# Sigmoid attention in bursts of seven energy tiles, with the values eight tiles behind

## The chip, the cores and the metric

The kernel runs on one core of a Trainium2 chip. The metric is device time in microseconds from the first to the last instruction of the program; lower is better. A core has a matrix engine (TensorE, "PE" in the profile, its weight loads "PEld"), a vector engine (VectorE, "DVE"), an engine for activation functions (ScalarE, "ACT"), a general one (GpSimd, "POOL"), and a sequencer that issues transfers ("SP"). Matmuls write to PSUM, which has eight banks of 512 float32 per partition; everything else lives in SBUF, with 128 partitions.

## The reference

The input x has 4 images of 64 channels and 96 x 96 positions (9216). Two layers follow one another, each added to its own input; `_gn` normalizes groups of two channels.

```python
q = einsum('bchw,oc->bohw', x, wq) + bq      # 8 channels
k = einsum('bchw,oc->bohw', x, wk) + bk      # 8 channels
v = einsum('bchw,oc->bohw', x, wv) + bv      # 64 channels
energy = einsum('bcn,bcm->bnm', Q, K)        # 9216 x 9216 per image
att = sigmoid(energy)
out = einsum('bcm,bnm->bcn', V, att) + x
scale = sigmoid(mlp(mean(out)) + mlp(max(out)))
layer0 = out * scale
...
x = x + layer0(_gn(x))
x = x + layer1(_gn(x))
```

Layer 1 takes a two-dimensional Fourier transform of the normalized x, multiplies the 32 x 16 lowest frequencies by a complex 64 x 64 matrix each (the spectral weights), and transforms back.

## The kernel before

The four images are two pairs p; the 64 channels of a pair's two images fill 128 partitions. The attention of a pair is cut into 18 blocks of 512 queries (NBLK), so there are 36 blocks in all. The keys are cut into 72 chunks of 128 (NCH). One **tile** is the energies of one chunk of one image against the block's 512 queries: a matmul (L424) with 32 contracted rows and 128 columns of weights that fills one PSUM bank. Queries and keys are held in four groups of 32 rows, and successive tiles take successive groups (`r = 32 * (t % 4)`). A block has 144 tiles. A sigmoid on ScalarE (L428) turns energies in PSUM into attention in SBUF (`at`). Then each **pair** of tiles (one chunk, both images) is multiplied by the values `vT` (L435): two matmuls of 64 columns each, which fill the two halves of the output `acc`, one bank, over all 72 chunks. Values and attention are full float32, which the profile shows as two matmul records, two passes, per matmul; the energies are float32r, one record.

The work is cut into **bursts** of six tiles (BURST), 24 a block, 864 in all. Six PSUM banks hold the energies, as two tensors `eb[0]`, `eb[1]` of three banks (PART); one sigmoid works on each. The loop over bursts t does: energies of burst t+1 and their two sigmoids, the side work listed in `mid[t]`, the three value pairs of burst t, the next block's queries in the fourth burst from a block's end, and the side work in `end[t]`; after a block's last burst, two vector instructions add `acc` to x and take a maximum (L578, L580). The remaining two PSUM banks form the pool `ps_a`: one holds `acc`, the other is used by side work, through `bank_a`.

Side work is all that isn't attention. In block 0 it makes keys and values of pair 0 a chunk of 512 at a time; in blocks 1 to 13 it takes statistics of pair 1 and normalizes it; in block 17 it makes pair 1's keys and values. From block 18 on, layer 1 of pair 0 runs as side work (class `Hidden`): `result` (combine with the gate, L158), `transposes` (L262), `along_w` (L272), `stats_steps`, `along_h` (L299), `mix` (L199), `back_h` (L318) and `back_w` (L339). Each is put at a fixed burst by `place(offset, every, steps)`. For `mix`, the weights of four of the 32 frequency rows are loaded into four buffers (`l1.weights`, L310) every ten bursts from burst 100 of pair 1 on; `mix(q, 0)` follows six bursts later and `mix(q, 1)` three after that. Each `mix(q, 1)` also stores its result (L215). After the attention, layer 1 of pair 1 runs as a tail, with nothing beside it.

The order in which instructions stand on each engine's queue follows the program's order, save where the framework that places them takes one that it reckons to be ready ahead of one that isn't. `later` keeps a step behind a marked vector instruction on its engine. Semaphores are put in by the framework from what each instruction reads and writes.

Of the kernel before, what the change touches and what calls it, by code (L numbers as in the profile page):

```python
# [33 lines left out]
F32 = mybir.dt.float32  # L34
F32R = mybir.dt.float32r
AF = mybir.ActivationFunctionType
ALU = mybir.AluOpType
AX = mybir.AxisListType
PSUM = bass.MemoryType.PSUM

P = 128
B, C, H, W = 4, 64, 96, 96
N = H * W
NPAIR = B // 2
# [3 lines left out]
KH = 32  # L48
NB = 512
NBLK = N // NB  # L50
NCH = N // P
BURST = 6
PART = 3
BURSTS = 2 * NCH // BURST
SIDE = 4
U = KH * KW * 4
UPAD = 4 * SIDE
STRIP = 8 * W
SQ = 32
NSQ = H // SQ  # L60
NSTRIP = N // STRIP
# [16 lines left out]
def tile_kernel(ctx: ExitStack, tc: tile.TileContext, x, cst, late, spec, out):  # L78
    nc = tc.nc
# [10 lines left out]
    xs = []  # L90
    for p in range(NPAIR):
        xt = xpool.tile([P, N], F32, tag=f"x{p}", name=f"x{p}")
        for s in range(9):
            cols = bass.ts(s, N // 9)
# [137 lines left out]
    class Hidden(Layer1):  # L232
# [25 lines left out]
        def transposes(self, r):  # L258

            pt = self.bank(f"pt_{self.p}_{r}")  # L260
            for i in range(4):
                nc.tensor.transpose(pt[:W, bass.ts(i, P)], xs[self.p][:, bass.ts(4 * r + i, W)],  # L262
                                    ident)
            self.xts[r] = self.work.tile([W, NB], F32, tag="xT", bufs=5, name=f"xT_{self.p}_{r}")
            self.move(self.xts[r], pt[:W, :])

        def along_w(self, m):
# [78 lines left out]
    with tc.tile_pool(name="work", bufs=1) as work, \  # L346
            tc.tile_pool(name="kv", bufs=1) as kvp, \
            tc.tile_pool(name="q", bufs=2) as qp, \
            tc.tile_pool(name="att", bufs=2) as attp, \
            tc.tile_pool(name="ps_s", bufs=1, space=PSUM) as ps_s, \  # L350
            tc.tile_pool(name="ps_a", bufs=2, space=PSUM) as ps_a:

        eb = [ps_s.tile([P, PART, NB], F32, tag=f"e{i}", name=f"e{i}") for i in range(2)]

        kT = kvp.tile([P, NCH // 2, P], F32R, tag="kT", name="kT")

        def bank_a(name):
            return ps_a.tile([P, NB], F32, tag="a", name=name)

        def halves(src, bias, name):  # L360

# [7 lines left out]
        mark = [None]  # L369
# [6 lines left out]
        def later(step):  # L376
            with tc.issue_after(mark[0].ins):
                step()
# [12 lines left out]
        def values_of(p, s):  # L391
            pp = bank_a(f"pv_{p}_{s}")
            for i in range(4):
                nc.tensor.matmul(pp[:, bass.ts(i, P)], xs[p][:, bass.ts(4 * s + i, P)],  # L394
                                 named("wv"), start=True, stop=True)
            nc.vector.tensor_tensor(  # L396
                vT[:, 4 * s:4 * s + 4, :], pp.rearrange("p (i m) -> p i m", m=P),
                named("bv").unsqueeze(1).to_broadcast([P, 4, P]), ALU.add)
# [16 lines left out]
                    nc.vector.tensor_copy(q[to:to + 32, cols], q[of:of + 32, cols])  # L415
            return q

        def energies(p, n, g, q):


            for i in range(BURST):
                t = BURST * g + i
                r = 32 * (t % 4)
                nc.tensor.matmul(eb[i // PART][:, i % PART, :], kT[r:r + 32, t // 4, :],  # L424
                                 q[r:r + 32, :], start=True, stop=True)
            at = attp.tile([P, BURST, NB], F32, tag="att", name=f"at_{p}_{n}_{g}")
            for h in range(BURST // PART):
                nc.scalar.activation(at[:, bass.ts(h, PART), :], eb[h], AF.Sigmoid)  # L428
            return at

        def attend(acc, g, at):
            for i in range(BURST):
                j, b = (BURST * g + i) // 2, i % 2
                half = slice(b * C, (b + 1) * C)
                nc.tensor.matmul(acc[half, :], vT[:, j, half], at[:, i, :],  # L435
                                 start=(j == 0), stop=(j == NCH - 1))

        def stats_of(p):

# [43 lines left out]
        q = queries(0, 0)  # L483
# [2 lines left out]
        keys(0, 1)  # L486
        values_of(0, 1)

        T = NPAIR * NBLK * BURSTS
        mid = [[] for _ in range(T)]  # L490
        end = [[] for _ in range(T)]
        for s in range(2, NBLK):
            end[s - 2] += [lambda s=s: keys(0, s)]
            mid[s - 1] += [lambda s=s: values_of(0, s)]
            if s + 1 < NBLK:
                end[s - 2] += [lambda s=s: later(norm0[s + 1])]
        each, norm1, mv1 = stats_of(1)
        for i, step in enumerate(each + norm1):
            end[(2 + i // 3) * BURSTS + 2] += [lambda step=step: later(step)]
        last = (NBLK - 1) * BURSTS  # L500
        for s in range(NBLK):
            t = last + -(-(4 * s + 1) // 3)
            end[t] += [lambda s=s: keys(1, s)]
            mid[t + 1] += [lambda s=s: values_of(1, s)]

        first = NBLK * BURSTS

        def place(offset, every, steps):
            for i, step in enumerate(steps):
                end[first + offset + every * i] += [lambda step=step: later(step)]  # L510

        gate, steps, _ = after(0)
        place(2, 2, steps)
        l1 = Hidden(0, gate, bank_a, lambda dst, src: nc.vector.tensor_copy(dst, src), work)  # L514
        x1d = dram.tile([P, N], F32, tag="x1", name="x1d")
        place(9, 3, [lambda s=s: (l1.result(s), nc.sync.dma_start(
            x1d[:, bass.ts(s, STRIP)], xs[0][:, bass.ts(s, STRIP)])) for s in range(NSTRIP)])
        place(13, 2, [lambda r=r: l1.transposes(r) for r in range(H // 4)])
        place(22, 8, [lambda m=m: l1.along_w(m) for m in range(H // 16)])
        place(64, 2, l1.stats_steps())  # L520

        def workspace():
            ws = xpool.tile([P, N], F32, tag="x0", name="ws")
            l1.ut = ws[:, :U + UPAD]
            at = 2080
            l1.wts = [ws[:, at + 1024 * i:at + 1024 * (i + 1)] for i in range(4)] * (KH // 4)
            l1.vms = [ws[:, at + 4096:at + 5120]] * (KH // 4)
            l1.z = ws[:, at:at + 3072].rearrange("q (h m) -> q h m", m=P)

        place(76, 1, [workspace])  # L530
        place(80, 4, [lambda i=i: l1.along_h(i) for i in range(4)])
        place(98, 1, [l1.constant_mode])
        place(100, 10, [lambda q=q: l1.weights(range(4 * q, 4 * q + 4)) for q in range(KH // 4)])
        for half in range(2):
            place(106 + 3 * half, 10, [lambda q=q, half=half: l1.mix(q, half)
                                       for q in range(KH // 4)])
        place(200, 3, [lambda i=i: l1.back_h(i // 4, i // 2 % 2, i % 2) for i in range(8)])
        place(244, 3, [lambda i=i: l1.back_w(i, x1d) for i in range(H // 4)])


        early = []
# [4 lines left out]
            for i, w in enumerate(early):  # L546
                nc.gpsimd.dma_start(w, spec[NSLOT + i])

        place(340, 1, [fetch])
        again = vT.rearrange("p j m -> p (j m)")  # L550
        for s in range(NSTRIP):
            end[T - BURSTS + 2 * s + 1] += [lambda s=s: nc.sync.dma_start(
                again[:, bass.ts(s, STRIP)], xf[bass.ts(1, P), bass.ts(s, STRIP)])]

        at = energies(0, 0, 0, q)
        qn = None
        for t in range(T):
            p, n, g = t // (NBLK * BURSTS), t // BURSTS % NBLK, t % BURSTS
            nxt = None
            if t + 1 < T:  # L560
                p1, n1, g1 = (t + 1) // (NBLK * BURSTS), (t + 1) // BURSTS % NBLK, (t + 1) % BURSTS
                if g1 == 0:
                    q = qn
                nxt = energies(p1, n1, g1, q)
            for step in mid[t]:
                step()
            if g == 0:
                acc = bank_a(f"acc_{p}_{n}")
            attend(acc, g, at)
            at = nxt  # L570
            if g == BURSTS - 4 and t + 4 < T:
                m = t // BURSTS + 1
                qn = queries(m // NBLK, m % NBLK)
            for step in end[t]:
                step()
            if g == BURSTS - 1:
                blk = xs[p][:, bass.ts(n, NB)]
                nc.vector.scalar_tensor_tensor(blk, acc, 1.0, blk, ALU.mult, ALU.add,  # L578
                                               accum_out=sums[p][:, n:n + 1])
                mark[0] = nc.vector.tensor_reduce(maxs[p][:, n:n + 1], blk, AX.X, ALU.max)  # L580
        gate, steps, f = after(1)
        for step in steps:
            step()
# [2 lines left out]
    with tc.tile_pool(name="tail", bufs=1, reuse_waits="tile") as tail, \  # L586
# [49 lines left out]
        for s in range(NSTRIP):  # L636
# [9 lines left out]
                pa = pa_bank.tile([P, 2 * NB], F32, tag="a", name=f"pa_{n}", bufs=2)  # L646
            v = xt.rearrange("q (h n c) -> q n h c", n=NSQ, c=SQ)
            for k in range(NSQ):
                last = nc.tensor.matmul(pa[:, bass.ts(i, STRIP // NSQ)], fw[:, bass.ts(k, P)], v[:, k],  # L649
                                 start=(k == 0), stop=(k == NSQ - 1))  # L650
            if i < NSTRIP // NSQ - 1:
                continue

# [73 lines left out]
        z = tail.tile([P, P, SQ], F32, tag="z", name="z_1")  # L727
        for i in range(4):
            for b in range(2):
                nc.vector.transpose(z[:H, b * C + i * NO:b * C + (i + 1) * NO, :], pz[b][i][:H, :].rearrange(  # L730
                    "q (k o) -> q o k", o=NO))
        banks.close()
        py_bank = psum("ps_y", 2)
        occupy(2, last, py_bank)
# [100 lines left out]
```

## Time and profile before

| what | value |
| --- | --- |
| time, median of 3 runs | 3196.64 us (3194.6 to 3197.18) |
| span of the profiled execution | 3196.5 us |
| mean granted TensorE clock | 0.995 |
| first energy matmul | 29.9 us after the start |
| last value matmul ends | 3106.0 us |
| ScalarE, of which idle before sigmoids | 2432.9 us busy, 682.8 us idle |
| VectorE busy | 396.4 us |

A line of the profile's groups reads: line of the kernel, engine, operation, tiles written and read, shapes, count, then busy time in us and the mean length of one in ns, then idle time of the engine before it and what ended it. A matmul's length is from its start to a modelled end, and matmuls overlap, so two of them take less than the sum. A line of the timeline reads: start in us, length in us of the merged instructions, then as above. Windows give, for each stretch, the busy time of each engine with the instruction count, the granted clock, the share of the transfer engines and GB/s.

### The profile page before, as it was taken

The page shows a single profiled execution, that of the slowest core. Times are in us where ns is not written, and L with a number is a line of the kernel's source. Part 1 is how long each engine was busy: PE and PEld are TensorE (multiplying, and loading weights), DVE is VectorE, ACT ScalarE, POOL GpSimd, SP SyncE. Part 2 cuts the span into 40 slices and gives each one's busy share as a digit, 9 for nine tenths or more (in the row PEclk, how much of TensorE's full clock was granted, in tenths as well). Part 3 has the DMA queues.
Part 4 walks back from the last instruction along what each step waited for, and adds up shares of the span by engine and source line. Part 5 has one row for each costly group of instructions (what it writes and reads, how often), then busy time and mean ns, then how long its engine had stood idle before and what let it go on. Part 6 is the DMA issues. An engine that isn't in the chain of part 4 may idle for free.

```text
span 3196.5 us, 39125 instructions
## 1 busy us (share of the span) xinstructions
PE 3153.5 (99%) x17490; PEld 1070.9 (34%) x17490; DVE 396.4 (12%) x838; ACT 2432.9 (76%) x1765; POOL 24.5 (1%) x49
## 2 busy tenths in 40 slices
PE   6999999999999999999999999999999999999998
PEld 3333333333333333334333333333333333333336
DVE  4200000000000000002331100000000111000015
ACT  3688888888888888886677777777777777888871
POOL 0000000000000000000000000000000000000001
PEclk9999999999999999999999999999999999999998
DMA  3000000000000000000120100121020102100026
GB/s 139 1 1 1 1 1 1 1 1 1 1 1 1 1 1 1 1 1 1 37 92 17 40 1 30 63 89 37 13 28 10 40 30 70 66 1 1 6 62 221
DMA packets 39145, 88.63 MB, mean 28 GB/s; under 512 B 10336, under 2 KB 17248, under 8 KB 38880
## 3 DMA queue, kind: packets, MB, share of 16 engines
q1 hardware_dynamic: 31856, 61.88, 6.4%
q0 software_dynamic: 5344, 19.27, 1.7%
q10 hardware_dynamic: 1776, 4.97, 0.4%
q8 instruction: 137, 2.24, 0.3%
q14 instruction: 32, 0.26, 0.0%
HBM read 62.77 MB, written 23.33 MB: 27 GB/s over the span
## 4 chain that ended last, share of the span: by engine, by line
PE 98%; DVE 1%; DMA 1%; issue 0%; ACT 0%; POOL 0%; SPq 0%; ACTq 0%
PE acc L435 74%; PE e L424 18%; PE pv L394 1%; PE pv L199 1%; PE py L339 1%; PE pq L405 1%; PE pk L385 1%; DMA x<-in_x_dram 0%; PE py L742 0%; PE pt L262 0%; DVE x L158 0%; DVE xt L641 0%; PE pz L318 0%; PE pu L299 0%; PE pa L272 0%
## 5 line engine op out<-in xcount | busy, mean ns | idle before, releaser
L428 ACT ACTIVATE at<-e 128x1536 f32<-128x1536 f32 x1728 | 2412.6, 1448 | 682.8 <-PE e L424 682.7
L435 PE MATMUL acc<-at,vT 128*64 128x512 f32 x10368 | 2418.1, 601 | 0.0
L435 PEld LDWEIGHTS acc<-at,vT 128*64 128x64 f32 x10368 | 667.8, 136 | 1294.7 <-issue 1279.3
L424 PE MATMUL e<-q,kT 32*128 32x512 f32 x5184 | 636.0, 461 | 1.8 <-ACT at L428 1.3
L424 PEld LDWEIGHTS e<-q,kT 32*128 32x128 f32 x5184 | 257.5, 182 | 642.8 <-issue 595.3
L365 DVE TENSOR_SCALAR full_q<-pq,cs 128x256 f32<-128x256 f32 x36 | 17.4, 484 | 1557.1 <-PE pq L405 1557.0
L578 DVE SCALAR_TENSOR_TENSOR x<-acc,x 128x512 f32<-128x512 f32 x36 | 24.9, 692 | 294.1 <-PE acc L435 294.1
L394 PE MATMUL pv<-cs,x 128*128 128x128 f32 x288 | 42.9, 292 | 0.1
L415 DVE CAST q<-q 32x256 fp32r<-32x256 f32 x144 | 41.0, 285 | 3.8
L341 DVE TENSOR_TENSOR x<-py,x 128x384 f32<-128x384 f32 x24 | 13.4, 558 | 226.0 <-PE py L339 226.0
L394 PEld LDWEIGHTS pv<-cs,x 128*128 128x128 f32 x288 | 35.7, 195 | 14.3 <-DVE full_k L365 12.9
L514 DVE COPY ws<-pv 128x512 f32<-128x512 f32 x16 | 11.1, 691 | 216.4 <-PE pv L199 216.3
L373 DVE SCALAR_TENSOR_TENSOR q<-high_q,cs,full_q 64x256 fp32r<-64x256 f32 x72 | 34.6, 480 | 2.4
L514 DVE COPY xT<-pt 96x512 f32<-96x512 f32 x24 | 16.4, 685 | 114.7 <-PE pt L262 114.7
L365 DVE TENSOR_SCALAR full_k<-pk,cs 128x256 f32<-128x256 f32 x36 | 17.4, 484 | 103.0 <-PE pk L385 103.0
L396 DVE TENSOR_TENSOR vT<-pv,cs 128x512 f32<-128x512 f32 x36 | 24.9, 691 | 8.8 <-PE pv L394 8.8
L580 DVE TENSOR_REDUCE maxs<-x 128x1 f32<-128x512 f32 x36 | 24.7, 685 | 1.1
L385 PE MATMUL pk<-x,cs 128*64 128x256 f32 x144 | 23.3, 395 | 1.5 <-DVE x L145 1.5
L442 DVE BATCH_NORM_STATS2 stats<-x 128x6 f32<-128x512 f32 x36 | 22.3, 679 | 8.1 <-DMA x<-in_x_dram 8.1
L649 PE MATMUL pa<-xt,lc 128*128 128x256 f32 x72 | 19.1, 425 | 3.7 <-DVE xt L641 2.6
L405 PE MATMUL pq<-x,cs 128*64 128x256 f32 x144 | 22.1, 386 | 0.0
L128 PE MATMUL pm_l<-mv_l,cs 128*128 128x1 f32 x8 | 1.7, 286 | 20.6 <-DVE mv_l L124 19.9
(104 smaller groups left out, 457.9 us busy)
## 6 DMA issues: line engine op xcount, KB each, us to landing
ws<-in_spec_dram SPq DMA_DIRECT2D x32, 512.0 KB
x<-in_x_dram SPq DMA_DIRECT2D x15, 512.0 KB
out_dram<-x SPq DMA_DIRECT2D x18, 384.0 KB
w<-in_spec_dram POOLq DMA_DIRECT2D x10, 512.0 KB, 6.6
old<-in_x_dram SPq DMA_DIRECT2D x12, 384.0 KB
x1d<-x SPq DMA_DIRECT2D x12, 384.0 KB
x<-x1d SPq DMA_DIRECT2D x12, 384.0 KB
w_early<-in_spec_dram POOLq DMA_DIRECT2D x9, 512.0 KB, 9.9
```

Of the source, the lines that this page charges most:

```text
L199: self.last = nc.tensor.matmul(pv[bass.ts(g, 32), :].rearrange("q (n k o) -> q n k o", n=SIDE, o=C)[:, :, k, :], self.ut[:, at:at + 32], s ...
L339: nc.tensor.matmul(py[:, :4 * W], self.z[:, i, :], named("gw"), start=True, stop=True)
L365: nc.vector.tensor_scalar(u, src, bias, None, ALU.add)
L373: mark[0] = nc.vector.scalar_tensor_tensor(dst, h.bitcast(F32), is_low, u, ALU.mult, ALU.add)
L385: nc.tensor.matmul(pp[cols, :NB // 2], named("wk")[:, cols], src[:, e, :, :], start=True, stop=True)
L394: nc.tensor.matmul(pp[:, bass.ts(i, P)], xs[p][:, bass.ts(4 * s + i, P)], named("wv"), start=True, stop=True)
L405: nc.tensor.matmul(pq[rows, :half], named("wq")[:, rows], xs[p][:, n * NB + e * half:n * NB + (e + 1) * half], start=True, stop=True)
L415: nc.vector.tensor_copy(q[to:to + 32, cols], q[of:of + 32, cols])
L424: nc.tensor.matmul(eb[i // PART][:, i % PART, :], kT[r:r + 32, t // 4, :], q[r:r + 32, :], start=True, stop=True)
L428: nc.scalar.activation(at[:, bass.ts(h, PART), :], eb[h], AF.Sigmoid)
L435: nc.tensor.matmul(acc[half, :], vT[:, j, half], at[:, i, :], start=(j == 0), stop=(j == NCH - 1))
L514: l1 = Hidden(0, gate, bank_a, lambda dst, src: nc.vector.tensor_copy(dst, src), work)
```

## The change

Bursts now have six or seven tiles, listed by block: DENSE blocks (0 and 17) have 24 sixes; the twelve HALF blocks from 18 to 29 have 22 bursts, ten of six and twelve of seven; all other blocks, SPARSE, have 21, three of six and eighteen of seven. The eight banks are one tensor. A block's `acc` is bank 7 or bank 0 by turns, the other end bank is the spare one for side work, and a burst of seven takes the spare bank too. Sigmoids work on the last three tiles of a burst and on those before them (three or four). Attention lives in one ring of 14 tiles. Values run eight tiles (LAG) behind the energies: the step that makes burst t+1 multiplies as many tiles as burst t+1 has, ending eight short of the energies made; where that is an odd number, a pair is split into halves of 256 queries. The next sigmoids are issued after those pairs of the step that touch the burst before last, and ahead of the others. Side work that uses a bank is put into `mid` of steps whose next burst has six tiles, one a step (`put`), over the twelve HALF blocks. The weights of the next four frequency rows are loaded right after `mix(q, 1)`. There are four xT buffers instead of five.

```diff
-BURST = 6
-PART = 3
-BURSTS = 2 * NCH // BURST
+DENSE = [6] * 24
+HALF = [6 if i == 1 or i % 2 == 0 and i < 18 else 7 for i in range(22)]
+SPARSE = [6 if i in (0, 1, 11) else 7 for i in range(21)]
+LAG = 8
...
-        eb = [ps_s.tile([P, PART, NB], F32, tag=f"e{i}", name=f"e{i}") for i in range(2)]
+        banks = ps_s.tile([P, 8, NB], F32, tag="banks", name="banks")
+        spare = [0]
+        at = attp.tile([P, 14, NB], F32, tag="at", name="at")
...
+        def bank_of(t):
+            return 0 if sizes[t] == 7 and block[t] % 2 == 0 else 1
+        def place(i):
+            t = burst[i]
+            return 7 * (t % 2 + 1) - sizes[t] + i - total[t - 1]
+        def sigmoids(t):
+            of, bank, size = 7 * (t % 2 + 1) - sizes[t], bank_of(t), sizes[t]
+            for lo, hi in ((0, size - 3), (size - 3, size)):
+                nc.scalar.activation(at[:, of + lo:of + hi, :], banks[:, bank + lo:bank + hi, :],
+                                     AF.Sigmoid)
+        def values_times(t):
+            h = done[t - 1]
+            while h < done[t]:
+                n = 1 if h % 2 or h + 1 == done[t] else 2
+                yield h // 2, slice(h % 2 * NB // 2, (h % 2 + n) * NB // 2)
+                h += n
...
+        pattern = [DENSE] + [SPARSE] * (NBLK - 2) + [DENSE] + [HALF] * 12
+        pattern += [SPARSE] * (NPAIR * NBLK - len(pattern))
+        done = [total[t + 1] - LAG for t in range(T - 1)] + [total[T - 1], 0]
+        free = [t for t in range(begins[1], T - 1) if sizes[t + 1] == 6 and t not in begins]
...
-        place(100, 10, [lambda q=q: l1.weights(range(4 * q, 4 * q + 4)) for q in range(KH // 4)])
-        for half in range(2):
-            place(106 + 3 * half, 10, [lambda q=q, half=half: l1.mix(q, half)
-                                       for q in range(KH // 4)])
-        place(200, 3, [lambda i=i: l1.back_h(i // 4, i // 2 % 2, i % 2) for i in range(8)])
-        place(244, 3, [lambda i=i: l1.back_w(i, x1d) for i in range(H // 4)])
+        def mixing(q, half):
+            l1.mix(q, half)
+            if half and q + 1 < KH // 4:
+                l1.weights(range(4 * q + 4, 4 * q + 8))
+        t = put(t + 1, [lambda q=q, half=half: mixing(q, half)
+                        for q in range(KH // 4) for half in range(2)])
+        t = put(t + 5, [lambda i=i: l1.back_h(i // 4, i // 2 % 2, i % 2) for i in range(8)])
+        t = put(t + 5, [lambda i=i: l1.back_w(i, x1d) for i in range(H // 4)])
...
-        place(340, 1, [fetch])
+        end[t + 30] += [fetch]
...
+                energies(t + 1, q)
             for step in mid[t]:
                 step()
+            items = list(values_times(t))
+            old = sum(1 for pair, _ in items if t and 2 * pair < total[t - 1])
+            attend(items[:old])
+            if t + 1 < T:
+                sigmoids(t + 1)
+            attend(items[old:])
```

## The prediction

> **What bounds the kernel now.** I read first the page's busy shares, then its chain of waits, then its costliest groups, to learn which engine sets the end:
>
> ```profile
> PE 3153.5 (99%) x17490; PEld 1070.9 (34%) x17490; DVE 396.4 (12%) x838; ACT 2432.9 (76%) x1765; POOL 24.5 (1%) x49
> ...
> PE acc L435 74%; PE e L424 18%; PE pv L394 1%; PE pv L199 1%; PE py L339 1%; PE pq L405 1%; PE pk L385 1%; DMA x<-in_x_dram 0%; PE py L742 0%; PE pt L262 0%; DVE x L158 0%; DVE xt L641 0%; PE pz L318 0%; PE pu L299 0%; PE pa L272 0%
> ...
> L428 ACT ACTIVATE at<-e 128x1536 f32<-128x1536 f32 x1728 | 2412.6, 1448 | 682.8 <-PE e L424 682.7
> L435 PE MATMUL acc<-at,vT 128*64 128x512 f32 x10368 | 2418.1, 601 | 0.0
> ...
> L424 PE MATMUL e<-q,kT 32*128 32x512 f32 x5184 | 636.0, 461 | 1.8 <-ACT at L428 1.3
> L424 PEld LDWEIGHTS e<-q,kT 32*128 32x128 f32 x5184 | 257.5, 182 | 642.8 <-issue 595.3 <-ACT at L428 46.0 <-DVE q L415 0.7
> ```
>
> TensorE is busy throughout and its two attention lines make 92% of the chain. ScalarE has 683 us of idle time, all of it waiting for TensorE. So what counts is the TensorE time of one burst; it is read from the timeline of matmuls, and of ScalarE, in a quiet place (start, length, line, count):
>
> ```profile
> 1002.50 0.73 PE L424 MATMUL e<-q,kT 32*128 32x512 f32 x6
> 1003.15 2.80 PE L435 MATMUL acc<-at,vT 128*64 128x512 f32 x12
> 1005.88 0.73 PE L424 MATMUL e<-q,kT 32*128 32x512 f32 x6
> 1006.54 0.65 PE L435 MATMUL acc<-at,vT 128*64 128x512 f32 x2
> ...
> 1003.10 2.79 ACT L428 ACTIVATE at<-e 128x1536 f32<-128x1536 f32 x2 [0.59 <-PE e L424]
> ```
>
> A period is 3.385 us (the next energies begin at 1009.27, two periods after 1002.50). From the first energy to the first value matmul it is 0.66 us, from there to the next energies 2.73. The twelve value matmuls are three pairs; each pair is two passes with the two halves of the array side by side, and the weight loads show the passes 0.43 us apart (1003.64, 1004.07, 1004.50, 1004.92). Six passes of 0.4285 are 2.57 us. What doesn't grow with the values is 3.385 - 2.57 = **0.815 us a burst**. Within the 0.66 the six energies start as four at once and two more 0.34 us later (single records), since tiles rotate over four row groups.
>
> **What the skill says.** The Trainium skill, "TensorEngine Tiling (Array Packing)", Key Properties, says that changing the tiling mode drains TensorE; a burst does that twice (32x128 to 128x64 and back). The trace agrees: a value pass is 0.43 us, but from the last pass's start to the next energies it is 0.53. The same page, Instruction Overhead, gives each matmul about 60 cycles, which would speak against half pairs. The trace does not charge it for 256 columns: the passes of the query projection, 128*64 with 256 columns, start 0.216 us apart, half of 0.43. "ScalarE: Activation LUTs", What ACT_TABLE_LOAD costs, gives an ACTIVATE 186 ns + 0.833 N ns, back-to-back ones overlapping by 93 ns: 1466 and 1373 for N=1536; the trace has 1448 for one and 1347 start to start. Close, so the form is usable for N=2048.
>
> **The change, part by part.**
>
> *Fewer bursts.* Before: 36 blocks of 24, 864. After: 2 blocks of 24, 12 of 22, 22 of 21: 48 + 264 + 462 = 774. So 90 bursts go. Value passes stay the same in sum. Does a burst of seven have the same 0.815? Energies are then four and three, still two rounds, the third matmul in a row group that stood empty. I take yes, bounded by 0.02 us more each (one more weight load, records 3 ns apart; the second round ends no later). Gain 90 x 0.815 = **73.4 us**; with 0.02 on the 540 bursts of seven (22 x 18 + 12 x 12) it would be 63.
>
> *Half pairs.* About 340 pairs are split (I followed the lag of eight through the burst sizes: 340 of 774 steps end on an odd tile). Each turns two passes of 0.4285 into four of 0.2155: 0.005 us, 1.7 us in all. Taken: **+2 us**.
>
> *Sigmoids of four and three banks.* N=2048 isn't in the trace. From its own numbers: 1347 ns start to start at 1536, plus 512 x 0.833 = 427, is 1774 ns; the skill's form gives 1800. A burst of seven then has ScalarE from 0.61 us after its first energy (1967.12 to 1967.73 for a burst that didn't wait) to 0.61 + 1.774 + 1.446 = 3.83. The next burst's fifth energy needs that; its weight load waits 0.05 for the semaphore, 3.88. TensorE gets there at 0.815 + 7 x 0.4285 = 3.815 for the burst plus 0.11 for the weight load's own place: 3.92. So it fits by 0.04 us, and by some 0.09 before the fifth energy itself, which starts 0.34 after the first, is late. Before, the fourth energy came 0.06 late by this same wait (the 46 us above) at no cost: the fifth still started 0.34 us after the first. Cost taken 0; the other end is ScalarE 0.1 us slower, 540 x 0.05 = 27 us.
>
> *Lag of eight, one ring of 14 tiles.* The second sigmoid overwrites tiles that the first value pair of the step still reads. That pair ends about 1.9 us after the first energy (0.66 + 0.48 + 0.74 from the last pass's start to a reader's); ScalarE reaches the instruction at 0.61 + 1.35 = 1.96 (six) or 2.39 (seven). It hides by 0.07 in bursts of six. Cost 0. At the ends, the first step has two tiles fewer and the last two more: nothing net.
>
> *Side work moved between the energies and the values of steps whose energies are six, on one spare bank.* Matmuls and vector instructions are the same ones. A mix step cost 1.00 us of TensorE at the end of a step (1962.74 to 1967.12, 4.39 instead of 3.385); between energies and values it has as many mode changes. Its evacuation (0.69 us) has 2.7 us of values to hide in before a burst of seven needs that bank. A block's closing addition (L578, 0.69 us) has the step's two remaining value pairs (1.7 us) to hide in before its bank is written again. Taken +1, bounds -5 to +25 (a hundred moved steps, 0.25 each).
>
> *The loads of spectral weights.* This one has an exposed end. Before, the loads for row group q had six bursts before the first mix that reads them. Now they're issued with the mix before, and the next is two bursts on. What they take:
>
> ```profile
> 1967.20 0.35 SPq L310 DMA_DIRECT2D ws<-in_spec_dram  x1
> 1968.06 1.79 SPq L215 DMA_DIRECT2D vd<-ws  x4
> 1969.89 1.40 SPq L310 DMA_DIRECT2D ws<-in_spec_dram  x3
> ...
> 1973.00:1975.00 2.00, 2.00 (x14) 0.58 (x12) 0.00 (x0) 1.41 (x2) 0.00 (x0) 1.00 1.02 418
> 1975.00:1977.00 2.00, 2.00 (x12) 0.57 (x8) 0.00 (x0) 2.00 (x2) 0.00 (x0) 1.00 0.28 113
> ```
>
> The issues on SP (first three lines) stand after a mix that began on TensorE at 1966.12: one load, four stores of its result, three loads. The windows by two microseconds (last column GB/s) show traffic until about 1976.1. So weights are there 10.0 us after the mix before began. The skill's "DMA: Bandwidth & Descriptors", Specifications, gives a ceiling of 435 GB/s; the 418 here agrees, so 2.1 MB can't shrink below 4.8 us. The time between those mixes is now 1.0 + 2.73 + 0.66 + 3.155 + 0.66 = 8.2 us (7.75 where a block begins, both bursts being six). TensorE runs in order, so the values behind the waiting mix wait too, then the next sigmoids. 5 x (10.1 - 8.2) + 2 x (10.1 - 7.75) = 14 us, if the order is as written. It may not be: in the trace a side matmul stands between three energies at 1816.86 and three at 1817.83, so instructions are placed by an estimate of readiness, and values can go ahead of a mix. Ends 0 and 21 (stores all ahead of loads, 1 us more each). Taken **+10 us**. The other round trips have room: the inverse's coefficients took 8 us after the last mix and now have five bursts, over 19 us; the rearrangement behind the last return step took 10 us (2372.5 to 2382.9) and has nine bursts.
>
> *Buffers, prefetch, tail.* One xT buffer fewer: the four transposes of a group still have their four. The prefetch comes about 100 bursts before the end instead of 92. The tail after the last value matmul (3106 to 3196.5) and the start (30 us) are the same instructions. Cost 0, within 3.
>
> Sum: 3196.5 - 73.4 + 2 + 1 + 10 = 3136.1 against the profiled 3196.5; the median of the three runs, 3196.64, is the same within their 2.6 us. **Forecast 3136 us.**
>
> **Rivals.**
> *ScalarE takes over in bursts of seven* (or each seven costs more on TensorE). For: the margin is 0.04 to 0.09 us, and N=2048 across four banks is unseen. Against: the two readings of its duration differ by 26 ns. At 0.08 us lost in each of 540: 3136 + 43 = 3179 us.
> *Side work stalls in its new places* (banks, vector queue, loads at their high end): +25 and +21 instead of +1 and +10: 3171 us. For: a full bank must be emptied before every seven; against: TensorE had little waiting on VectorE with one free bank before.
> *The 46 us of weight-load waiting were real* and go with the new grouping: 3136 - 29 (its share in 540 of 864 bursts) = 3107. Against: the unchanged 0.34.
> *Slower: the ring is followed as one whole.* All attention tiles share one buffer now. If the first sigmoid of a burst must wait for the step's first value pair, not only the second one, it begins at 1.9 instead of 0.61 us; in a seven the fifth energy is then ready at 5.17 instead of 3.92, 1.25 us late, in a six 1.35: 540 x 1.25 + 234 x 1.35 = 991 us, 4127 us in all. It decides from a start later than about 0.7 us. Against: in the first block keys and values are written into slices of kT and vT beside reads of other slices without such a wait. The banks, too, are now one tensor; no row shows that tracked by bank.
>
> **How the numbers follow.** Forecast's case 0.58 (3122 to 3150), ScalarE 0.13, side stalls 0.12, earlier waits real 0.07, the ring 0.08, and 0.02 for gains eaten up. Bounds of the unknown costs with most of the two middle rivals give 3110 to 3172. 0.2% is 6.4 us, about what a measurement of this kernel can tell from no change: faster 0.88, same 0.03, slower 0.09, the tails of the ScalarE and stall cases giving the little beyond the ring's.
>
> **What would show it.** Right: 774 bursts; 3.81 to 3.82 us between bursts of seven; 0.66 from energies to values in both sizes; the sigmoid of 2048 at about 1.87 us; a gap before the mix (L199) matmuls of about 2 us, seven times. Wrong: a fifth energy more than 0.36 us behind the first; first sigmoids starting later than 0.65 us after their energies; value matmuls standing between energies.

## The result and the profile after

The changed kernel takes 3164.95 us (median of 3162.57 to 3166.1), the kernel before, with one run more than in the table above, 3196.59 us. The ratio is 0.9901, with a 95% interval of 0.9884 to 0.9918: faster by 1.0%. The forecast was 3136 us, its range 3110 to 3172. Of the gain that was forecast, 60 us, about half came: 31.6 us between the medians, 35.7 between the profiled executions (3196.5 and 3160.8, the second being the shortest of its four). The question is where the other half went.

On the page after, these lines answer to those shown of before: the busy time of the engines, the chain of waits, and the groups of the sigmoids, the values and the energies. The tensors `e` and `acc` are now both called `banks`; L461 is the values' line, L432 the energies'.

```profile
PE 3116.3 (99%) x18850; PEld 1157.4 (37%) x18850; DVE 397.7 (13%) x838; ACT 2424.2 (77%) x1585; POOL 24.5 (1%) x49
...
PE banks L461 74%; PE banks L432 16%; PE banks L401 1%; PE banks L203 1%; PE banks L412 1%; PE banks L343 1%; PE banks L392 1%; DMA x<-in_x_dram 0%; PE py L812 0%; PE pv L203 0%; PE banks L266 0%; DVE x L162 0%; DMA old<-in_x_dram 0%; DVE xt L711 0%; PE banks L322 0%; PE banks L303 0%
```

TensorE is as full as before, still 99%, and its chain is still the values and the energies. The energies' share fell from 18% to 16%. Nothing here says that anything is amiss; the gap to the forecast is not an idle engine.

The groups by shape show what the page merges, first the sigmoids of three and of four banks, then the values of whole and of half query blocks:

```profile
L461 PE MATMUL banks<-at,vT 128*64 128x512 f32 x9008 | 2105.8, 598 | 0.0
L443 ACT ACTIVATE at<-banks 128x1536 f32<-128x1536 f32 x1008 | 1445.7, 1447 | 289.9 <-PE banks L432 198.7 <-PE banks L461 91.0
L443 ACT ACTIVATE at<-banks 128x2048 f32<-128x2048 f32 x540 | 1013.7, 1877 | 366.4 <-PE banks L432 365.6 <-ACT at L443 0.8
...
L432 PE MATMUL banks<-q,kT 32*128 32x512 f32 x5184 | 577.6, 454 | 2.3 <-ACT at L443 1.2 <-DVE xT L579 1.2
L461 PE MATMUL banks<-at,vT 128*64 128x256 f32 x2720 | 431.3, 391 | 0.0
L432 PEld LDWEIGHTS banks<-q,kT 32*128 32x128 f32 x5184 | 235.1, 183 | 481.2 <-issue 304.1 <-ACT at L443 165.7 <-DVE maxs L468 4.9
```

There are 540 sigmoids of four banks, one for each burst of seven, and 2720 half matmul records, 8 for each of 340 split pairs. The sigmoid of 2048 elements takes 1877 ns. A quiet place in the timeline, matmuls and sigmoids:

```profile
1005.54 0.73 PE L432 MATMUL banks<-q,kT 32*128 32x512 f32 x7
1006.20 3.23 PE L461 MATMUL banks<-at,vT 128*64 128x512 f32 x16
1009.36 0.73 PE L432 MATMUL banks<-q,kT 32*128 32x512 f32 x7
...
1006.16 3.22 ACT L443 ACTIVATE at<-banks 128x2048 f32<-128x2048 f32 x2 [0.60 <-PE banks L432]
```

From energies to energies it is 3.82 us, from energies to values 0.66, and the sigmoids start 0.62 after the first energy: the picture that the prediction drew. So the steady state is right, and the loss sits elsewhere. The starts of successive blocks find it (a block's length is from its first energy to the next block's first, from single records):

| blocks | before, us | after, us | expected for fewer bursts | not expected |
| --- | --- | --- | --- | --- |
| 1 to 16, most of them | 81.7 | 79.4 | -2.4 | +0.1 |
| 17 | 106.5 | 108.2 | 0 | +1.8 |
| 18 to 22, sum | 444.1 | 425.9 | -8.1 | -10.1 |
| 23 to 25, sum | 258.2 | 298.6 | -4.9 | +45.3 |
| 26 to 31, sum | 519.1 | 507.0 | -11.4 | -0.7 |

Side work now stands in other blocks than before, so single rows of blocks 18 to 31 mix its move with its price. But blocks 23 to 25, where the mixes (L203) of the spectral weights are, stand out. The timeline of matmuls there:

```profile
2000.76 3.23 PE L461 MATMUL banks<-at,vT 128*64 128x256 f32 x16
2003.91 0.73 PE L432 MATMUL banks<-q,kT 32*128 32x512 f32 x6
2004.57 0.62 PE L203 MATMUL banks<-ws 128*32 128x256 f32 x2
2005.12 2.79 PE L461 MATMUL banks<-at,vT 128*64 128x512 f32 x10
2007.84 0.62 PE L203 MATMUL banks<-ws 128*32 128x256 f32 x2
2008.39 1.07 PE L461 MATMUL banks<-at,vT 128*64 128x512 f32 x2
2009.39 0.73 PE L432 MATMUL banks<-q,kT 32*128 32x512 f32 x5
2010.05 0.62 PE L203 MATMUL banks<-ws 128*32 128x256 f32 x2
2010.60 0.49 PE L432 MATMUL banks<-q,kT 32*128 32x512 f32 x1
2011.02 1.93 PE L461 MATMUL banks<-at,vT 128*64 128x512 f32 x6
2012.88 1.05 PE L203 MATMUL banks<-ws 128*32 128x256 f32 x10
2013.87 1.08 PE L461 MATMUL banks<-at,vT 128*64 128x512 f32 x4
2014.88 0.50 PE L432 MATMUL banks<-q,kT 32*128 32x512 f32 x1
```

A mix is 16 matmul records, and this one stands in pieces of 2, 2, 2 and 10. It takes four frequency rows; the first matmul of each of the first three stands alone, that of the fourth with all the rest, and other work fills in between. That is what comes of placing each where its weights are reckoned to be there; the reckoning itself is not in the record. The bursts around it have lost their shape as well: an energy alone at 2010.60 and at 2014.88, value pairs by one and two. TensorE has no gap here; in all seven such stretches it has one, 1.19 us before an energy at 2062.12, and none before a mix. From 2003.91 to the next whole burst (2021.34) it is 17.43 us. The whole bursts, mix and query in it come to 3.39 + 1.00 + 3.82 + 3.39 + 0.43 = 12.03, so 5.4 us are lost, by six pieces more than needed: three of the mix and three of energies (six runs of energies for three bursts). That is 0.9 us a piece on average. Seven mixes stand in pieces of 2, 2, 2 and 10.

### The profile page after: what moved, and what is told of

Same layout as the page of the kernel before. It is cut to its first block, busy times and chain, and to the rows that moved or that the text cites. A ratio compares the mean times of both kernels' runs of the same rounds, so it can differ in the third digit from the quotient of the medians.

```text
span 3160.8 us, 42345 instructions
## 1 busy us (share of the span) xinstructions
PE 3116.3 (99%) x18850; PEld 1157.4 (37%) x18850; DVE 397.7 (13%) x838; ACT 2424.2 (77%) x1585; POOL 24.5 (1%) x49
## 4 chain that ended last, share of the span: by engine, by line
PE 97%; DVE 1%; DMA 1%; issue 0%; ACT 0%; SPq 0%; POOL 0%; ACTq 0%; DVEq 0%
PE banks L461 74%; PE banks L432 16%; PE banks L401 1%; PE banks L203 1%; PE banks L412 1%; PE banks L343 1%; PE banks L392 1%; DMA x<-in_x_dram 0%; PE py L812 0%; PE pv L203 0%; PE banks L266 0%; DVE x L162 0%; DMA old<-in_x_dram 0%; DVE xt L711 0%; PE banks L322 0%; PE banks L303 0%
## 5 line engine op out<-in xcount | busy, mean ns | idle before, releaser
L443 ACT ACTIVATE at<-banks 128x1536 f32<-128x1536 f32 (+1 forms) x1548 | 2404.0, 1597 | 656.3 <-PE banks L432 564.3
L461 PE MATMUL banks<-at,vT 128*64 128x512 f32 (+1 forms) x11728 | 2415.9, 550 | 0.0
L461 PEld LDWEIGHTS banks<-at,vT 128*64 128x64 f32 x11728 | 777.1, 136 | 1361.3 <-issue 1303.6
L432 PE MATMUL banks<-q,kT 32*128 32x512 f32 x5184 | 577.6, 454 | 2.3 <-ACT at L443 1.2
L432 PEld LDWEIGHTS banks<-q,kT 32*128 32x128 f32 x5184 | 235.1, 183 | 481.2 <-issue 304.1
L466 DVE SCALAR_TENSOR_TENSOR x<-banks,x 128x512 f32<-128x512 f32 x36 | 24.9, 692 | 898.1 <-PE banks L461 898.1
L401 PE MATMUL banks<-cs,x 128*128 128x128 f32 x288 | 43.8, 297 | 1.5 <-DVE full_q L372 0.6
L401 PEld LDWEIGHTS banks<-cs,x 128*128 128x128 f32 x288 | 36.6, 199 | 16.2 <-DVE full_k L372 14.6
L579 DVE COPY xT<-banks 96x512 f32<-96x512 f32 x24 | 16.5, 686 | 167.4 <-PE banks L266 167.4
L203 PE MATMUL banks<-ws 128*32 128x256 f32 x256 | 30.0, 387 | 0.0
L392 PE MATMUL banks<-x,cs 128*64 128x256 f32 x144 | 23.9, 396 | 1.6 <-DVE x L149 1.5
L412 PE MATMUL banks<-x,cs 128*64 128x256 f32 x144 | 23.9, 410 | 0.6 <-DVE full_k L372 0.6
```

The source lines that it names most:

```text
L203: self.last = nc.tensor.matmul(pv[bass.ts(g, 32), :].rearrange("q (n k o) -> q n k o", n=SIDE, o=C)[:, :, k, :], self.ut[:, at:at + 32], s ...
L392: nc.tensor.matmul(pp[cols, :NB // 2], named("wk")[:, cols], src[:, e, :, :], start=True, stop=True)
L412: nc.tensor.matmul(pq[rows, :half], named("wq")[:, rows], xs[p][:, n * NB + e * half:n * NB + (e + 1) * half], start=True, stop=True)
L432: nc.tensor.matmul(banks[:, bank_of(t) + i - starts[t], :], kT[r:r + 32, i // 4, :], q[r:r + 32, :], start=True, stop=True)
L443: nc.scalar.activation(at[:, of + lo:of + hi, :], banks[:, bank + lo:bank + hi, :], AF.Sigmoid)
L461: nc.tensor.matmul(acc[half, cols], vT[:, j, half], at[:, place(2 * pair + b), cols], start=(j == 0), stop=(j == NCH - 1))
```

## The experiments

**Theory A**: the loads of weights, issued two bursts ahead of their use, break the mixes and the bursts around them, and the many small pieces with a change of tiling between them are the loss. **Theory B**: side work between energies and values, on one spare bank, costs that by itself. Runs are compared with the kernel before that ran on the same chip (3196.4 to 3196.6 us).

**Without the loads.** The mixes of rows 4 to 31 use the weights of the first four rows; the program leaves 28 loads of 0.5 MB out and is otherwise the changed kernel.

```diff
         def mixing(q, half):
             l1.mix(q, half)
-            if half and q + 1 < KH // 4:
-                l1.weights(range(4 * q + 4, 4 * q + 8))
```

> The changed kernel (3165 us) with 28 of the 32 loads of spectral weights left out; every mix reads the first four rows' weights again, nothing else is altered. Theory A (the loads, issued two bursts ahead, break each mix into four pieces that stand among values and energies, and so break bursts): one broken stretch of the changed kernel took 17.4 us where its whole bursts, mix and query come to 12.0, so 5.4 us for each of seven, 38 in all: about 3127 us, all mixes whole. Theory B (side work between energies and values costs this by itself, with or without loads): no less than 3155 us, and blocks 23 to 25 as long as before.

Measured: 3131.26 us (3130.54 to 3133.58), ratio 0.9796 (0.978 to 0.9812). All 16 mixes stand whole. The loads had cost 3164.95 - 3131.26 = **33.7 us**, 4.8 for each of seven mixes. Theory B falls: the side work is in the same places, and 34 us are gone.

**In order.** The values and the next energies are kept behind a mix on TensorE's queue, so that the mix waits whole.

```diff
             l1.mix(q, half)
+            held[0] = l1.last
...
+        def behind(step):
+            if held[0] is None:
+                return step()
+            with tc.issue_after(held[0].ins):
+                step()
...
-            attend(items[:old])
+            behind(lambda: attend(items[:old]))
```

> The changed kernel with the step's values and the next energies kept behind a mix on TensorE's queue, so that a mix waits whole for its weights. Theory A with the prediction's price for waiting in order: 3127 + 14 = 3141 us, seven gaps of about 2 us ahead of the first or second matmul of a mix. If waiting in order costs what the pieces cost: about 3165 us. If the pieces are a good bargain: above 3165.

Measured: 3154.27 us (3149.68 to 3156.3), ratio 0.9867 (0.9852 to 0.9881). The loads now cost 23.0 us, 10.7 less than in pieces. So waiting in order is the better bargain, and the pieces cost 10.7 us beyond the waits that they avoid. The price of waiting was put too low, though: 14 us. The timeline of one mix that waits, with idle time and its cause in brackets:

```profile
2005.10 0.73 PE L432 MATMUL banks<-q,kT 32*128 32x512 f32 x6
2005.76 0.63 PE L203 MATMUL banks<-ws 128*32 128x256 f32 x4
2006.65 0.62 PE L203 MATMUL banks<-ws 128*32 128x256 f32 x2 [0.27 <-DMA ws<-in_spec_dram]
2008.13 1.05 PE L203 MATMUL banks<-ws 128*32 128x256 f32 x10 [0.85 <-DMA ws<-in_spec_dram]
2009.11 2.37 PE L461 MATMUL banks<-at,vT 128*64 128x512 f32 x10
```

The mix before began at 1997.54, 8.22 us earlier, as reckoned. Its last weight packet ended 10.23 us after that start, and the matmul that needed it came at 10.59, 0.36 us after the packet. By the mixes' first and last records, the seven took 2.0 to 4.7 us longer than 0.69, 21.1 in all. The longest was `mix(4, 0)`, where four loads of `vt` (L233) run beside the weights and the last packet ended at 11.90.

The pieces did not even follow the weights. In the first broken mix of the changed kernel the first matmuls of the four rows start 8.2, 11.5, 13.7 and 16.5 us after the mix before began; here, where they wait, 8.2, 8.5, 9.1 and 10.6. In the changed kernel, too, the last weight packet of that mix ended after 10.3 us, before its second piece began. So the order, fixed ahead, allowed the loads more time than they took.

**Loads four bursts ahead.** A row's weights are laid out in two halves, one for each `mix(q, half)`. The half that a mix has read is loaded anew right behind that mix.

```diff
-                        self.wts[4 * q + g].rearrange("q (n k o) -> q n k o", n=SIDE, o=C)[
-                            :, :, kw, :], start=True, stop=True)
+                        self.wts[4 * q + g][:, bass.ts(half, KW * C // 2)].rearrange(
+                            "q (n k o) -> q n k o", n=SIDE, o=C)[:, :, k, :],
+                        start=True, stop=True)
...
-            if half and q + 1 < KH // 4:
-                l1.weights(range(4 * q + 4, 4 * q + 8))
+            if q + 1 < KH // 4:
+                l1.weights(range(4 * q + 4, 4 * q + 8), half)
...
```

> The changed kernel with each row's weights laid out in two halves, the half that a mix has just read being loaded anew right after that mix, so that a load is four bursts (15 us) ahead of its use instead of two. All loads are done. Theory A: mixes whole, about 3127 us, as without loads. Theory B: no less than 3155 us. If half rows (2 KB runs) load so slowly that 15 us don't hold them: 3135 to 3150.

Measured: 3132.9 us (3130.97 to 3134.82), ratio 0.9802 (0.9787 to 0.9816). All the loads are done and they cost nothing that can be told from leaving them out. From the mix that frees a half to the one that uses it anew it was 16.0 us or more. A second measurement, beside the changed kernel on one chip:

> The kernel with half-row loads once more, on the same chip as the one before: 3133 us, and 32 us under the changed kernel.

> The changed kernel itself once more, on the same chip as the other two of this call, for the comparison: 3165 us.

Measured: 3130.24 us (3128.43 to 3132.09) against 3163.66 (3162.19 to 3165.77), ratios 0.9791 (0.9778 to 0.9805) and 0.9898 (0.9885 to 0.9912). This version beats both kernels, by 33.4 and 66.3 us. Its timeline where a mix is, and its line of busy time:

```profile
2052.85 0.73 PE L434 MATMUL banks<-q,kT 32*128 32x512 f32 x6
2053.51 1.07 PE L203 MATMUL banks<-ws 128*32 128x256 f32 x16
2054.51 2.80 PE L463 MATMUL banks<-at,vT 128*64 128x256 f32 x16
...
PE 3087.1 (99%) x18850; PEld 1152.9 (37%) x18850; DVE 397.7 (13%) x838; ACT 2424.3 (77%) x1585; POOL 24.4 (1%) x49
```

The matmul count is that of the changed kernel, 18850, and the work is the same; busy time is 29 us less. The records' modelled ends run across the changes of tiling between pieces, so these count as busy.

**Mixes further apart.** The loads stay whole and stay where they are, but the next mix is put further behind (`+ 4`). Of the blocks of 22 bursts about every second step has room for side work, and queries take some, so the next mix came not four but six bursts or more behind, by the trace 22.6 to 45.6 us, instead of 7.8 to 8.2; one more block has 22 bursts, and the prefetch for the tail comes 8 bursts after the last return step instead of 30.

```diff
-        pattern = [DENSE] + [SPARSE] * (NBLK - 2) + [DENSE] + [HALF] * 12
+        pattern = [DENSE] + [SPARSE] * (NBLK - 2) + [DENSE] + [HALF] * 13
...
-        t = put(t + 1, [lambda q=q, half=half: mixing(q, half)
-                        for q in range(KH // 4) for half in range(2)])
+        t += 1
+        for qq in range(KH // 4):
+            t = put(t, [lambda q=qq, half=half: mixing(q, half) for half in range(2)]) + 4
+        t -= 4
...
```

> The changed kernel with whole rows loaded as it does, but the next mix(q+1, 0) four bursts behind mix(q, 1) instead of two, for which a thirteenth block gets 22 bursts (0.8 us), and the prefetch for the tail 8 bursts instead of 30 after the last return step. Theory A: mixes whole, 3132.9 + 0.8 = 3134 us. If it was the half rows' layout and not the distance that helped before: 3150 to 3165 us.

Measured: 3132.5 us (3131.32 to 3135.64), ratio 0.9802 (0.9787 to 0.9816), all mixes whole. Distance between load and use is enough; the layout is not needed.

**The breaking without bursts of seven.** In the kernel before, only the mixes are moved together, as they are in the changed kernel.

```diff
-        place(100, 10, [lambda q=q: l1.weights(range(4 * q, 4 * q + 4)) for q in range(KH // 4)])
+        place(100, 1, [lambda: l1.weights(range(4))])
+        place(109, 4, [lambda q=q: l1.weights(range(4 * q, 4 * q + 4)) for q in range(1, KH // 4)])
         for half in range(2):
-            place(106 + 3 * half, 10, [lambda q=q, half=half: l1.mix(q, half)
+            place(106 + 2 * half, 4, [lambda q=q, half=half: l1.mix(q, half)
                                        for q in range(KH // 4)])
```

> The kernel before (bursts of six, 3196.4 us) with only its mixes moved: mix(q, 1) two bursts after mix(q, 0), the loads of the next four rows issued with it, and mix(q+1, 0) two bursts on, as in the changed kernel; all else stays where it was. Theory A (loads too close to their use break the mixes and bursts, whatever the bursts' size): the 33.7 us that the changed kernel got back without its loads are lost here, about 3230 us, mixes in pieces of 2, 2, 2 and 10 matmul records. If the breaking hurts only beside bursts of seven or side work in the middle: below 3205 us.

Measured: 3222.59 us (3221.85 to 3223.82), ratio 1.0081 (1.0064 to 1.0098). That is 26.0 us lost, 3.7 for each of seven mixes: less than 33.7, but the greater part. Its timeline shows the same pieces of 2, 2, 2 and 10, here with side work behind the values:

```profile
1971.24 0.62 PE L199 MATMUL pv<-ws 128*32 128x256 f32 x2
1971.79 0.73 PE L424 MATMUL e<-q,kT 32*128 32x512 f32 x6
1972.45 1.93 PE L435 MATMUL acc<-at,vT 128*64 128x512 f32 x6
1974.31 0.62 PE L199 MATMUL pv<-ws 128*32 128x256 f32 x2
...
1977.15 0.62 PE L199 MATMUL pv<-ws 128*32 128x256 f32 x2
1977.69 0.51 PE L424 MATMUL e<-q,kT 32*128 32x512 f32 x4
1978.13 1.07 PE L435 MATMUL acc<-at,vT 128*64 128x512 f32 x2
1979.13 1.05 PE L199 MATMUL pv<-ws 128*32 128x256 f32 x10
```

So neither bursts of seven nor the place within a step is needed for it: loads two bursts ahead of their use are enough to break the mixes. One of the seven had 10.3 us from mix to mix and was broken too.

**Sixes in place of sevens.** The changed kernel with its 22 blocks of 21 bursts made blocks of 24 sixes.

```diff
-        pattern = [DENSE] + [SPARSE] * (NBLK - 2) + [DENSE] + [HALF] * 12
-        pattern += [SPARSE] * (NPAIR * NBLK - len(pattern))
+        pattern = [DENSE] + [DENSE] * (NBLK - 2) + [DENSE] + [HALF] * 12
+        pattern += [DENSE] * (NPAIR * NBLK - len(pattern))
```

> The changed kernel with all its blocks of 21 bursts made blocks of 24 sixes; the twelve blocks of 22, the side work and the loads stay. If the gain is the fixed price of a burst: 66 bursts x 0.815 = 53.8 us, less 396 sevens x 0.007 us that a seven costs beyond it: 3165 + 51 = 3216 us. If the gain came from the ring and the lag (waits of ScalarE or of weight loads going away): below 3195 us.

Measured: 3216.24 us (3213.61 to 3216.92), ratio 1.0061 (1.0046 to 1.0076): 51.3 us more than the changed kernel for 66 bursts, as reckoned. The blocks' bursts of six take 3.387 us (median), as in the kernel before, so the ring and the lag change nothing by themselves; the gain is the fixed price of a burst. With 840 bursts instead of 864 this kernel is still slower than the one before: the change's other parts, the loads above all, cost more than 24 bursts give.

**Three and four.** The version with half-row loads, with the two sigmoids of a burst of seven regrouped.

```diff
-            for lo, hi in ((0, size - 3), (size - 3, size)):
+            for lo, hi in ((0, 3), (3, size)):
```

> The kernel with half-row loads (3132.9 us) with the sigmoids of a burst of seven regrouped: three tiles first and four after, where four came first. Then the fourth energy of a burst, not the fifth, waits for the second sigmoid, which by the trace is ready 3.88 us after the burst's first energy, 0.05 after the fourth energy's place. By the prediction's reading (a fourth energy 0.06 late cost nothing in the kernel before): unchanged, within 4 us. If ScalarE's margin counts, 0.05 us in each of 540 bursts: about 3160 us.

Measured: 3140.25 us (3138.36 to 3140.57), ratio 0.9823 (0.9808 to 0.9838): 7.4 us more than the 3132.9 it started from, so neither of the two numbers. By the single records, the fourth energy of a seven starts 0.059 us after the first instead of 0.010, the fifth still at 0.338, and the median period of sevens is unchanged at 3.822. So a late fourth energy is free, as read. What cost was not foreseen: in even blocks, a six behind a seven has its third energy in a bank that the second sigmoid of the seven reads. It starts 0.058 us after the first instead of 0.007, and its own first sigmoid needs all three. In blocks 18 to 29, sixes behind sevens took 0.067 us longer in even blocks and 0.041 in odd ones, 5.1 us over 95 of them; why odd blocks took part wasn't traced. The mean period of sevens in the blocks of 21, up 0.005 us, gives 2 more.

**Results further apart.** One period in blocks 18 to 29, outside the mixes, was long: in block 19 a seventh energy waited for a copy on VectorE that empties the spare bank. The copy stood behind a combining step (L162) that waited 4.5 us for its strip. Here those steps are three bursts apart.

```diff
-            end[first + 7 + 2 * s] += [lambda s=s: later(lambda: (
+            end[first + 7 + 3 * s] += [lambda s=s: later(lambda: (
```

> The kernel with half-row loads, with the steps that combine a strip of x with the gate (L162) three bursts apart instead of two, so that a strip's old values have 11 us to arrive instead of 7. In block 19 VectorE waited 4.5 us for such a load, the copy that empties the spare bank stood behind it, and the seventh energy of a burst waited 1.23 us: that period was 3.4 us too long, the only such one in blocks 18 to 29. If the load's lateness is its cause: 3.4 us less than the kernel with half-row loads, about 3129.5, and no period with such an excess. If copies on VectorE are just slow there: no change.

Measured: 3130.49 us (3129.22 to 3131.42), ratio 0.9794 (0.978 to 0.9807), beside 3130.24 without it: no change. VectorE still waited 4.22 us at that place (VectorE's instructions first, then transfers issued by SP):

```profile
1618.23 1.02 DVE L162 SCALAR_TENSOR_TENSOR x<-x,gate,old 128x768 f32<-128x768 f32 x1 [1.84 <-DMA old<-in_x_dram]
1619.28 1.02 DVE L257 BATCH_NORM_STATS2 stats<-x 128x6 f32<-128x384 f32 x2
1624.52 1.02 DVE L162 SCALAR_TENSOR_TENSOR x<-x,gate,old 128x768 f32<-128x768 f32 x1 [4.22 <-DMA old<-in_x_dram]
1625.45 0.68 DVE L581 COPY xT<-banks 96x512 f32<-96x512 f32 x1
...
1619.27 0.34 SPq L585 DMA_DIRECT2D x1d<-x  x1
1619.66 0.43 SPq L254 DMA_DIRECT2D old<-in_x_dram  x1
```

The spacing was not the cause; SP's queue shows what makes the load late. The load of `old` (L254) that this step needs was issued at 1619.66, right behind the store of the strip before (L585), and that store waits for the strip's own combining step, 1618.23 + 1.02. So a load goes out only when the step before is done, and the next step waits for it: they followed one another by 6.3 us here, not by the three bursts of the program. The 4.9 us from issue to use were not taken apart. Nor is the excess steady: 3.4 and 1.4 us in two executions of the same program, 1.5 here.

## Why the prediction was right, and where not

**Fewer bursts: right.** 774 bursts, and the price of 0.815 us held: blocks of 21 are 2.3 us shorter (2.4 reckoned), and giving the 66 bursts back cost 51.3 us.

**Bursts of seven and half pairs: right in kind, 2 us short.** A seven takes 3.822 us, 0.0075 more than 0.815 + 7 x 0.4285 = 3.8145; over 540 that is 4.0 us. The 2 us taken for half pairs are in it. Of the extra, 0.003 us are between energies and values (0.664 instead of 0.661), the seventh energy's.

**ScalarE's margin: right.** The first sigmoid of a seven starts 0.62 us after the first energy, the second 1.773 later (1.774 was worked out), and the fifth energy is 0.338 behind the first in sixes and sevens alike. The sigmoid of 2048 took 1877 ns; the form in the Trainium skill, "ScalarE: Activation LUTs", What ACT_TABLE_LOAD costs, gives 1892. The rival in which ScalarE takes over did not come. The regrouping shows how near it is: 0.05 us of delay on the third energy of 47 bursts went with 3 us.

**The ring and the banks tracked as one whole: refuted by the same 0.62 us.** First sigmoids don't wait for a value pair, and values written to one bank don't wait for sigmoids that read others.

**The earlier waits: right that they were not real.** The idle time of the energies' weight loads that the groups put down to ScalarE rose from 46.0 to 165.7 us, with the fifth energy where it was and the period as reckoned.

**Side work: within its bounds.** Without the loads the changed kernel is 65.1 us faster than before (3196.36 to 3131.26). The steps for bursts, sevens and half pairs make 73.4 - 4.0 = 69.4. The 4 us left were put at +1. Block 17's 1.8 us and the single stall in block 19 (1.4 to 3.9 us in the executions traced, 3.9 in this run's) are of that size; they were not taken apart further.

**The loads of spectral weights: the step that failed.** It was put at +10 us, between 0 and 21, and measured 33.7 us. The place and the cause of lateness were right: 8.22 us from mix to mix (7.78 where both bursts are sixes, not 7.75), weights after 10.2. Two things were wrong.

The smaller is the price of waiting in order, 14 us: measured 23.0. The prediction read one of the seven loads and put its weights at 10.0 us. In the packets of the trace before, the seven end 10.0 to 11.0 us after the mix before began; in the run in order they end after 9.8 to 11.9, the longest beside the loads of `vt`. Beyond 10.0 that last run's seven make 4.5 us. A matmul started 0.34 to 0.71 us after the last packet where 0.1 was allowed, which makes 2.4. The 1.9 us of the 23.0 that are not in the mixes were not traced.

The larger is the sign of the escape. The prediction saw that the framework may place values ahead of a mix that is reckoned not to be ready, and took this for relief, the end at 0. It is the dearer way: four pieces instead of one, each among work of another tiling, with bursts of energies broken to match. What was reckoned as a wait is no wait in the profile at all. Of the signs that the prediction named, the gaps of 2 us before seven mixes did not come, and values between energies, a sign of being wrong, did.

Medians give the whole sum: -73.4 for bursts, +4.0 for sevens, +33.7 for the loads is -35.7, and -31.6 was measured, so some 4 us are left for side work, as above. That the profiled executions differ by 35.7 is chance. It is luck, too, that the time lies in the forecast's range: the loads alone went past their bound of 21, and the range held because the room that it kept for ScalarE and side work was hardly used.

## What to carry to other kernels

Where instructions are placed by reckoned readiness, a load that comes too late can show as small pieces instead of a gap, and busy time hides it. Look at the timeline for runs that should be whole, and compare blocks, not shares. Before moving steps closer together, check each transfer between them against the new distance. Here the weights were in place 9.6 to 12.5 us after the start of the mix that frees their buffers. Distances of 7.6 to 10.3 us broke the mixes; 16.0 us (half rows) and 22.6 us (whole rows) left them whole, and nothing between was tried. A burst's fixed price, read from one period as what doesn't grow with the work, predicted the gain of larger bursts within 3 us of 51.

## What the runs showed of the hardware

Pieces are dear: between value passes that are 0.43 us apart, one with two matmul records takes 0.52 to start, 0.24 from its first to its second pass, and 0.31 until the next value pass, 1.07 us instead of 0.43. A whole mix of 16 records costs 1.00.

Waiting in order for late weights beat working around them by 10.7 us over seven mixes (3154.27 and 3164.95).

A matmul that waited for a load started 0.34 to 0.44 us after the load's last packet in six mixes of the run in order, and 0.71 in the one where other loads followed.
